# Sorting one block's neighbour lists and starting each layer with its first 16 slots

## The chip, the cores and the metric

The kernel runs on one core of a Trainium2 chip. The metric is the device time of one execution in microseconds. Engines are called by the profile's names: PE is TensorE, DVE is VectorE, ACT is ScalarE, POOL is GpSimd, and SP issues transfers only.

## The reference

Eight graphs (B = 8) share one random adjacency matrix of 2048 nodes with a density of 0.0078125, so about 16 neighbours a node; each node has 128 features. Four layers follow one another: two of attention with 8 heads over the neighbours, then two in which the weights come from a sum of two scores.

```python
x, adj = ...            # (8, 2048, 128), (2048, 2048)
# layers 0 and 1
scores = jnp.einsum('bnhd,bmhd->bhnm', Q, K) / jnp.sqrt(16.)
scores = jnp.where(mask, -jnp.inf, scores)        # mask: adj == 0
attn_out = softmax(scores) @ V
x = layer_norm(h + (attn_out @ Wo + bo))
x = layer_norm(x + relu(x @ W1 + b1) @ W2 + b2)
# layers 2 and 3
e = s_i[:, :, None] + s_j[:, None, :]             # s = (x @ W) @ a
e = jnp.where(e >= 0, e, 0.2 * e)
att = softmax(jnp.where(adj == 0, -jnp.inf, e))
x = layer_norm(att @ (x @ W) + x)
```

## The kernel before

A node needs only its neighbours' rows. In the start phase the kernel finds each node's neighbours, counts them, and sorts the nodes by falling count: `perm` holds the node at every place, `rank` the place of every node. The 2048 places make 16 blocks of 128 nodes (one node a partition). Block t has `CAPS[t]` neighbour slots, 28 in block 0 and 11 in block 15; the first 16 nodes of block 0 may have more, and 2 folded slots, spread over all partitions, take these. `find_lists` (L328) makes a block's list, by falling node number. `verdict` looks at all the limits at the end (`over` among them), and where one is broken, a general path computes everything anew.

Each layer l has a table in DRAM, `tables[l]`, with one row per node: keys and values of all 8 graphs for layers 0 and 1 (2048 numbers), features and two scores for layers 2 and 3 (1040). A slot of a block is one indirect DMA that GpSimd issues (`gather`, L299): 128 rows, one for each partition. Two slots make a chunk in layers 0 and 1, four in layers 2 and 3. Six buffers `kv0` to `kv5` hold chunks in turn; a chunk is fetched three chunks ahead of its use (four in layers 2 and 3: `AHEAD`).

A chunk of layers 0 and 1 is multiplied with the query on DVE (L528), reduced to scores (L531), turned into weights on ACT (L537), the values are multiplied on DVE (L542), and PE adds them into PSUM (L552). A chunk of layers 2 and 3 has small weight operations (L667 to L673), a multiply on DVE (L679), two of eight graphs on ACT (L684), an addition of pairs of slots (L688) and the sum on PE (L694).

When a block's last chunk is through, `outputs` (L565 or L571) multiplies the sums by the reciprocal of the weights' sums. Then the block's tail runs in two halves of four graphs each, on PE and ACT with one power on POOL for each norm (L411, in `normed`): projections and norms, then `project` computes the rows of the next layer's table, and `put_rows` (L419) writes them with an indirect DMA of POOL. `state_done` also stores the block's transposed state with a DMA of SP (L480) and starts the load (L295) of the state of the block three further on.

The order of the instructions on every engine is the order in which the program emits them. Tails are generators that give way at fixed points; each chunk's step has three slots, and in a slot every pending tail is taken one part further:

```python
def slot():
    advance(threads)
    advance(tails)
```

A layer ends with `drain`, which takes the tails to their end. Only then does the next layer's first fetch follow:

```python
for i in range(AHEAD[l]):
    fetch(i)
if l > 0:
    state(0)
drain()
begin(0)
drain()
```

Of the kernel before, what the change touches and what calls it, by code (L numbers as in the profile page):

```python
# [31 lines left out]
AHEAD = (3, 3, 4, 4)  # L32
# [6 lines left out]
CAPS = [BASE + FOLD, 23, 21, 20, 19, 18, 18, 17, 16, 16, 15, 14, 14, 13, 12, 11]  # L39
SEG = 128  # L40
# [12 lines left out]
def pieces(t, n):  # L53

    res, k = [], 0
    for m in split(CAPS[t] if t > 0 else BASE, n):
        res.append((k, m, False))
        k += m
    if t == 0:
        res.insert(1, (BASE, FOLD, True))  # L60
    return res
# [3 lines left out]
def sparse_path(ctx: ExitStack, tc: tile.TileContext, ins: dict, out: bass.AP, flag: bass.AP):  # L65
# [69 lines left out]
    first = [sum(CAPS[:t]) for t in range(NT)]  # L135

# [161 lines left out]
    def gather(l, at, dst):  # L298
        nc.gpsimd.indirect_dma_start(  # L299
            out=dst, out_offset=None, in_=tables[l][:, :],  # L300
            in_offset=bass.IndirectOffsetOnAxis(ap=lists[:, at : at + 1], axis=0),
            bounds_check=N - (l < 2), oob_is_err=False,
        )
# [72 lines left out]

    def folded_sums(w, box):
# [22 lines left out]
    def normed(z, dst):  # L400
# [15 lines left out]
        yield  # L416

# [56 lines left out]
    def state_done(l, t, box):  # L474
# [3 lines left out]
        if box["halves"] == 2:  # L478
# [3 lines left out]
            box["state"](t + 3)  # L482
# [257 lines left out]
    def start():  # L740
# [159 lines left out]
        nc.vector.tensor_add(perm, part1, pn[:, NT : 2 * NT])  # L900

# [35 lines left out]

    def advance(group):
        for g in list(group):
            if next(g, 0) == 0:  # L940
                group.remove(g)

    def slot():
        advance(threads)
        advance(tails)

# [5 lines left out]
    def tail(l, t, box):  # L952
        def rest():
            for _ in range(2 if l < 2 else 3):
                yield
            outputs(l, t, box)
            part = attention_tail if l < 2 else gat_tail
            tails.append(part(l, t, box, 0))
            tails.append(later(3, lambda: part(l, t, box, 4)))
            yield  # L960

        tails.append(rest())

# [5 lines left out]
    def layer(l):  # L969
        boxes = [{} for _ in range(NT)]  # L970
        att = l < 2
        per = 2 if att else 4
        chunks = []
        for t in range(NT):
            for k, ns, folded in pieces(t, per):
                chunks.append(dict(t=t, k=k, ns=ns, folded=folded, box=boxes[t], last=False))
            chunks[-1]["last"] = True
        n = len(chunks)

        def fetch(c):  # L980
            if c >= n:
                return
            c = chunks[c]
            c["buf"] = buffer()[:, : c["ns"] * width(l)].rearrange("p (s c) -> p s c", s=c["ns"])
            for i in range(c["ns"]):
                gather(l, first[c["t"]] + c["k"] + i, c["buf"][:, i])

        def state(t):
            if t < NT:
                if l == 0:  # L990
                    threads.append(fetch_state(t, boxes[t]))
                else:
                    boxes[t].update(x=load_state(t), ready=True)

        for box in boxes:
            box["state"] = state

        def begin(t):
            if att:
                threads.append(attention_begin(l, t, boxes[t]))  # L1000

        if l == 0:
            threads.append(find_lists(0))
            state(0)
            drain()
        for i in range(AHEAD[l]):
            fetch(i)
        if l > 0:
            state(0)
        drain()  # L1010
        begin(0)
        drain()
        if l == 0:
            threads.append(find_lists(1))
        run = [(attention_chunk if att else gat_chunk)(l, c) for c in chunks]

        def go(i, times=1):

            if 0 <= i < n:
                for _ in range(times):  # L1020
                    next(run[i], None)

        def is_last(i):
            return 0 <= i < n and chunks[i]["last"]

        def end(i):
            t = chunks[i]["t"]
            tail(l, t, chunks[i]["box"])

        for i in range(n + 2):  # L1030
            fetch(i + AHEAD[l])
            if i < n and chunks[i]["k"] == 0:
                t = chunks[i]["t"]
                if l == 0 and t + 2 < NT:
                    threads.append(find_lists(t + 2))
                if t == 0:
                    state(1)
                    threads.append(later(12, lambda: state(2) or iter(())))
                while att and "asked" not in chunks[i]["box"]:
                    advance(threads)  # L1040
            if i + 2 < n and chunks[i + 2]["k"] == 0:
                begin(chunks[i + 2]["t"])
            if att:

                go(i - 2)
                if is_last(i - 2):
                    end(i - 2)
                go(i)
                slot()
                go(i)  # L1050
                slot()
                if is_last(i - 1):
                    sums(l, chunks[i - 1]["t"], chunks[i - 1]["box"])
                go(i - 1, 2)
                slot()
            else:


                if i + 1 < n and chunks[i + 1]["folded"]:
# [544 lines left out]
```

## Time and profile before

| | |
|---|---|
| Time, median of 3 runs | 3458.94 us (3458.14 to 3458.99) |
| Span of the profiled execution | 3460.6 us |
| DVE busy | 3055.0 us, 88% |
| PE busy | 2749.7 us, 79% |
| POOL busy | 2125.4 us, 61% |
| ACT busy | 1435.0 us, 41% |
| Gathers (L299) | 1108, 1622.8 us on POOL |
| Power of the norm (L411) | 192, 318.2 us on POOL |
| Table writes (L419) | 48, 73.8 us on POOL |
| DMA, mean | 283 GB/s |

Busy times are sums over the whole span. Layers 0 and 1 take about 2100 us of it, layers 2 and 3 about 1180, and the stages have different limits, so the shares of the whole say little of any one of them. The time from a table's last write to the first use of its rows is seen in the timelines around 1217 to 1280 us, 2277 to 2340 and 2842 to 2889. POOL's records cover the issue of a gather, not its transfer.

### The profile page before, as it was taken

Reading aid. Unit: us, or ns where it says so; the run is one execution under the profiler, and the core shown is the slowest. Engines: PE = TensorE matmul, PEld = TensorE weight load, DVE = VectorE, ACT = ScalarE, POOL = GpSimd, SP = SyncE. Lnnn points to the kernel's source line nnn. Section 1 sums busy time; section 2 is a strip of 40 time slices with the busy share of each in tenths; the row PEclk is TensorE's granted clock in tenths of the full one; section 3 lists DMA queues with packets and bytes.
Section 4 is the critical chain, followed back from the end, with each engine's and each line's share of the span. In section 5 each row is a group of like instructions: output and inputs, shape, how many; then the busy total and the mean of one; then the engine's idle time right before and its main releaser. Section 6 shows DMA issues by size and latency. Waiting matters only on the chain. (4 is left out here: it accounts for less than half of the span.)

```text
span 3460.6 us, 34591 instructions
## 1 busy us (share of the span) xinstructions
PE 2749.7 (79%) x10618; PEld 1587.6 (46%) x10618; DVE 3055.0 (88%) x2685; ACT 1435.0 (41%) x4972; POOL 2125.4 (61%) x1441
## 2 busy tenths in 40 slices
PE   5657888799899966888888989975888995668675
PEld 4523455455555542444555556652444552223332
DVE  7789999999999929999999999938888875888886
ACT  5612333344344440233333434443555663444444
POOL 0053666666667533555677766628878756888874
PEclk9878999899999989989999999998999997988888
DMA  8486778888878547777887888729999967989883
GB/s 339 179 306 248 282 280 299 321 294 304 315 295 313 211 167 281 266 295 294 307 299 306 293 305 304 283 69 337 334 327 346 336 266 275 321 301 317 299 292 123
DMA packets 195887, 980.13 MB, mean 283 GB/s; under 512 B 28334, under 2 KB 30128, under 8 KB 124084
## 3 DMA queue, kind: packets, MB, share of 16 engines
q0 software_dynamic: 172352, 884.08, 70.2%
q1 hardware_dynamic: 18438, 75.51, 5.7%
q10 hardware_dynamic: 4904, 18.24, 1.4%
q8 instruction: 87, 1.43, 0.2%
q14 instruction: 106, 0.87, 0.1%
HBM read 937.13 MB, written 85.21 MB: 295 GB/s over the span
## 5 line engine op out<-in xcount | busy, mean ns | idle before, releaser
L299 POOL DMA_INDIRECT kv<-table,lists x1108 | 1622.8, 1465 | 523.7 <-issue 240.9
L552 PE MATMUL acc<-kv,ident 128*128 128x512 f32 x2200 | 1110.6, 636 | 257.7 <-DVE kv L542 257.4
L694 PE MATMUL acc<-kv,ident 128*128 128x512 f32 x1184 | 610.2, 664 | 236.7 <-DVE kv L688 191.1
L552 PEld LDWEIGHTS acc<-kv,ident 128*128 128x128 f32 x2200 | 413.4, 201 | 698.6 <-issue 368.2
L528 DVE TENSOR_TENSOR kv<-kv,q 128x2048 f32<-128x2048 f32 (+1 forms) x282 | 629.3, 2232 | 69.5 <-DMA kv<-table,lists 63.3
L531 DVE TENSOR_REDUCE sc<-kv 128x128 f32<-128x2048 f32 (+1 forms) x284 | 634.1, 2233 | 9.4
L411 POOL TENSOR_TENSOR rs<-ss,half 128x4 f32<-128x4 f32 x192 | 318.2, 1657 | 518.2 <-ACT n L406 517.1
L542 DVE TENSOR_TENSOR kv<-kv,w 128x2048 f32<-128x2048 f32 (+1 forms) x284 | 631.4, 2223 | 0.0
L406 ACT ACTIVATE n<-m,eps 128x128 f32<-128x128 f32 x768 | 271.9, 367 | 544.6 <-PE m L634 216.8
L694 PEld LDWEIGHTS acc<-kv,ident 128*128 128x128 f32 x1184 | 240.1, 213 | 543.3 <-issue 295.8
L679 DVE TENSOR_TENSOR kv<-kv,pair 128x3072 f32<-128x3072 f32 (+1 forms) x150 | 466.2, 3108 | 0.9
L684 ACT ACTIVATE kv<-kv,ws 128x128 f32<-128x128 f32 x1108 | 339.0, 403 | 189.2 <-DVE ws L673 86.8
L688 DVE TENSOR_TENSOR kv<-kv 128x2048 f32<-128x2048 f32 (+1 forms) x150 | 296.0, 1974 | 110.5 <-ACT kv L684 104.9
L537 ACT ACTIVATE w<-sc,lmask 128x64 f32<-128x64 f32 x554 | 164.6, 349 | 521.5 <-DVE sc L531 406.9
L415 ACT ACTIVATE n<-m,rs 128x128 f32<-128x128 f32 x768 | 219.6, 369 | 328.6 <-POOL rs L411 321.9
L406 ACT ACTIVATION_READ_ACCUMULATOR n<-m,eps 128x1 f32 x768 | 157.2, 205 | 0.0
L634 PE MATMUL m<-w_L_w,hT 128*128 128x128 f32 x1024 | 156.3, 275 | 0.0
L308 PE MATMUL m<-ident,n 128*128 128x128 f32 x640 | 105.9, 286 | 46.2 <-ACT n L415 45.7
L419 POOL DMA_INDIRECT table<-rows,perm x48 | 73.8, 1537 | 104.4 <-ACT rows L443 46.0
L634 PEld LDWEIGHTS m<-w_L_w,hT 128*128 128x128 f32 x1024 | 135.0, 192 | 0.0
L613 PE MATMUL m<-n1T,w_L_gnn_W 128*128 128x512 f32 x256 | 131.3, 597 | 3.3 <-ACT n1T L608 3.3
L308 PEld LDWEIGHTS m<-ident,n 128*128 128x128 f32 x640 | 81.6, 146 | 103.4 <-ACT n L415 49.9
(219 smaller groups left out, 3029.5 us busy)
## 6 DMA issues: line engine op xcount, KB each, us to landing
kept<-xT SPq DMA_DIRECT2D x48, 512.0 KB
xT<-kept SPq DMA_DIRECT2D x48, 512.0 KB
kv<-table,lists POOLq DMA_INDIRECT x1108
kv<-in_adj_dram SPq DMA_DIRECT2D x16, 1024.0 KB
table<-kv ACTq DMA_DIRECT2D x16, 1024.0 KB
kv<-in_x_nodes_dram SPq DMA_DIRECT2D x16, 512.0 KB
found<-cand POOLq DMA_DIRECT2D x16, 64.0 KB
table<-rows,perm POOLq DMA_INDIRECT x48
```

Of the source, the lines that this page charges most:

```text
L299: nc.gpsimd.indirect_dma_start(out=dst, out_offset=None, in_=tables[l][:, :], in_offset=bass.IndirectOffsetOnAxis(ap=lists[:, at : at + 1] ...
L406: nc.scalar.activation(dst[:, i, :], z[:, i, :], AF.Square, bias=eps, scale=D**-0.5, accum_out=ss[:, i : i + 1],)
L411: nc.gpsimd.tensor_tensor(rs, ss, half, op=ALU.pow)
L528: nc.vector.tensor_mul(kk, kk, q[:, None].to_broadcast([P, ns, NB, D]))
L531: nc.vector.tensor_reduce(sc[:, :ns].rearrange("p s (b h) -> p (s b) h", h=NH), kk.rearrange("p s b (h j) -> p (s b) h j", h=NH), axis=AX. ...
L542: nc.vector.tensor_mul(vv, vv, w[:, k : k + ns, :].rearrange("p s (b h) -> p (s b) h", h=NH)[:, :, None, :] .to_broadcast([P, ns * NB, HD, ...
L552: nc.tensor.matmul(acc[:, j, :], merge if c["folded"] else ident, kv[:, i, 4 * j : 4 * j + 4, D:], start=k + i == 0, stop=c["last"] and i ...
L634: nc.tensor.matmul(y[:, j, :], hT[:, f, j, :], wt["2"][:, f, :], start=False, stop=f == 1, skip_group_check=True,)
L679: nc.vector.tensor_mul(hv[:, :, :nv, :], hv[:, :, :nv, :], wc[:, :, :nv, None].to_broadcast([P, ns, nv, D]))
L684: nc.scalar.mul(hv[:, i, b, :], hv[:, i, b, :], ws[:, i, b - nv : b - nv + 1])
L688: nc.vector.tensor_add(hv[:, : ns - left], hv[:, : ns - left], hv[:, left:ns])
L694: nc.tensor.matmul(acc[:, j, :], merge if c["folded"] else ident, hv[:, i, 4 * j : 4 * j + 4, :], start=k + i == 0, stop=c["last"] and i = ...
```

## The change

One list of chunks, `every`, now runs through all four layers, and `layers` walks it without a drain between layers. `fetch` asks of each chunk how many blocks' rows must have been written to its layer's table (`put[l]`): all 16 as a rule. For block 0 of layers 1 to 3 there is a second list, `lists0`, with the same 28 neighbours ordered by their place in `perm`. Chunks within its first 8 slots ask for 14 blocks, chunks within its first 16 slots for 15. The folded chunk of these blocks moves from second place to behind slot 16.

`order_lists` makes `lists0` during layer 0, from block 2 on: `rank` is stored to DRAM in the start phase, 28 indirect gathers of one number per partition fetch the places (one a chunk), and DVE sorts keys made of place and node. Two more limits go into `over`: the 8th neighbour must not be in the last two blocks and the 16th not in the last one. `clear_late` writes zeros to the rows of blocks 14 and 15 in the tables of layers 1 to 3, with six `put_rows` during layer 0's first block.

`hurry` is true in block 15 of layers 0 to 2 and as long as a layer's table lacks rows that its chunks use; then a slot advances the tails twice. `state` passes from a layer's last blocks to the next layer's first, so these states are loaded as the blocks 13 to 15 are done. Where a chunk hasn't been fetched when its turn comes, slots go on without it until it has.

```diff
-AHEAD = (3, 3, 4, 4)
...
+EARLY = (8, 16)
...
-def pieces(t, n):
+def pieces(t, n, at):

     res, k = [], 0
     for m in split(CAPS[t] if t > 0 else BASE, n):
         res.append((k, m, False))
         k += m
     if t == 0:
-        res.insert(1, (BASE, FOLD, True))
+        res.insert(at, (BASE, FOLD, True))
...
+    lists0 = const.tile([P, BASE], I32, name="lists0")
+    ranks = dram.tile([N, 1], F32, name="ranks")
...
+    def order_lists():
+        place = small.tile([P, BASE], F32, tag="place", name="place", bufs=1)
+        nc.vector.memset(place, float(N))
+        for k in range(BASE):
+            nc.gpsimd.indirect_dma_start(
+                out=place[:, k : k + 1], out_offset=None, in_=ranks[:, :],
+                in_offset=bass.IndirectOffsetOnAxis(ap=lists[:, k : k + 1], axis=0),
+                bounds_check=N - 1, oob_is_err=False,
+            )
+            for _ in range(3):
+                yield
+        for _ in range(6):
+            yield
+        key = small.tile([P, 32], F32, tag="key", name="key", bufs=1)
+        nc.vector.memset(key, 0.0)
+        nc.vector.scalar_tensor_tensor(
+            key[:, :BASE], place, -4096.0, lists[:, :BASE], op0=ALU.mult, op1=ALU.subtract
+        )
+        nc.vector.tensor_scalar_add(key[:, :BASE], key[:, :BASE], float(4097 * N))
+        top = small.tile([P, 48], F32, tag="top", name="top")
+        for r in range(0, 32, 8):
+            nc.vector.max(top[:, r : r + 8], key)
+            if r < 24:
+                nc.vector.match_replace(key, top[:, r : r + 8], key, 0.0)
+        yield
+        for i, b in zip(EARLY, (2, 1)):
+            late = small.tile([P, 1], F32, tag="late", name="late", bufs=1)
+            nc.vector.tensor_single_scalar(
+                late, top[:, i - 1 : i], float(4096 * (b * P + 1)), op=ALU.is_lt
+            )
+            nc.vector.scalar_tensor_tensor(
+                over[:, 1, 0:1], top[:, i - 1 : i], late, over[:, 1, 0:1],
+                op0=ALU.mult, op1=ALU.max,
+            )
+        nc.vector.tensor_copy(lists0, top[:, :BASE])
+        nc.vector.tensor_single_scalar(lists0, lists0, 4095, op=ALU.bitwise_and)
+        nc.vector.tensor_scalar(
+            lists0, lists0, -1.0, float(N), op0=ALU.mult, op1=ALU.add
+        )
+        yield
...
+    def clear_late():
+        rows = rows_of(blocks[0][0])
+        nc.vector.memset(rows, 0.0)
+        for l in (1, 2, 3):
+            for t in (NT - 2, NT - 1):
+                for _ in range(3):
+                    yield
+                put_rows(l, t, rows)

...
+                put[l + 1] += 1
+            state(l, t + 3)

...
+        nc.sync.dma_start(ranks.rearrange("(t p) o -> p (t o)", p=P), rank)
...
+    put = [NT, 0, 0, 0]
+    every = []
+    blocks = [[{} for _ in range(NT)] for _ in range(4)]
+    for l in range(4):
+        per = 2 if l < 2 else 4
+        for t in range(NT):
+            for k, ns, folded in pieces(t, per, 1 if l == 0 else EARLY[1] // per):
+                c = dict(l=l, t=t, k=k, ns=ns, folded=folded, box=blocks[l][t], last=False)
+                c["run"] = (attention_chunk if l < 2 else gat_chunk)(l, c)
+                every.append(c)
+            every[-1]["last"] = True
+    now = [0, 0]
+    def fetch():
+        while now[1] < len(every):
+            c = every[now[1]]
+            l, t, k, ns = c["l"], c["t"], c["k"], c["ns"]
+            if now[1] - now[0] > (4 if now[1] >= KVB and every[now[1] - KVB]["l"] > 1 else 3):
+                return
+            need = NT
+            if l > 0 and t == 0 and not c["folded"]:
+                need -= (k + ns <= EARLY[0]) + (k + ns <= EARLY[1])
+            if put[l] < need:
+                return
+            c["buf"] = buffer()[:, : ns * width(l)].rearrange("p (s c) -> p s c", s=ns)
+            for i in range(ns):
+                if l > 0 and t == 0 and not c["folded"]:
+                    index = lists0[:, k + i : k + i + 1]
+                else:
+                    index = lists[:, first[t] + k + i : first[t] + k + i + 1]
+                gather(l, index, c["buf"][:, i])
+            now[1] += 1
+    def hurry():
+        c = every[min(now[0], len(every) - 1)]
+        return c["l"] < 3 and c["t"] == NT - 1 or c["l"] > 0 and put[c["l"]] < NT
     def slot():
         advance(threads)
         advance(tails)
+        if hurry():
+            advance(tails)
+        fetch()

...
+    def tail(l, t, box):
+        for _ in range(2 if l < 2 else 3):
+            yield
+        outputs(l, t, box)
+        part = attention_tail if l < 2 else gat_tail
+        n = 1 + hurry()
+        tails.append(later(n, lambda: part(l, t, box, 0)))
+        tails.append(later(n + 3, lambda: part(l, t, box, 4)))
+        yield
+    def state(l, t):
+        if t >= NT:
+            l, t = l + 1, t - NT
+        if l == 0:
+            threads.append(fetch_state(t, blocks[l][t]))
+        elif l < 4:
+            blocks[l][t].update(x=load_state(t), ready=True)
...
+    def layers():
+        threads.append(find_lists(0))
+        state(0, 0)
+        drain()
+        fetch()
+        begin(every[0])
+        drain()
+        threads.append(find_lists(1))
+        for i in range(len(every) + 2):
+            now[0] = i
+            fetch()
+            c2, c1, c, n1, n2 = (chunk(i + j) for j in range(-2, 3))
+            if c["k"] == 0:
+                l, t = c["l"], c["t"]
                 if l == 0:
+                    if t + 2 < NT:
+                        threads.append(find_lists(t + 2))
+                    if t == 0:
+                        state(0, 1)
+                        threads.append(later(12, lambda: state(0, 2) or iter(())))
+                        threads.append(later(12, clear_late))
+                    if t == 2:
+                        threads.append(order_lists())
+                while l < 2 and "asked" not in c["box"]:
+                    slot()
+            while i < len(every) and now[1] <= i:
                 slot()
+            if n2["k"] == 0:
+                begin(n2)
+            if c2["l"] in (0, 1):
+                go(c2)
+                if c2["last"]:
+                    threads.append(tail(c2["l"], c2["t"], c2["box"]))
+            if n1["l"] in (2, 3) and n1["folded"]:
+                go(n1)
+            if c1["l"] in (2, 3) and c1["last"]:
+                sums(c1["l"], c1["t"], c1["box"])
+            go(c)
+            slot()
+            go(c)
+            slot()
+            if c1["l"] in (0, 1) and c1["last"]:
+                sums(c1["l"], c1["t"], c1["box"])
+            go(c1, 2)
+            if c1["l"] in (2, 3) and c1["last"]:
+                threads.append(tail(c1["l"], c1["t"], c1["box"]))
+            slot()
+        verdict()
```

More of the change, by code (lines that the diff above doesn't have):

```diff
@@ L296, in load_state, with gather @@
         return xT
-    def gather(l, at, dst):
+    def gather(l, index, dst):
         nc.gpsimd.indirect_dma_start(
             out=dst, out_offset=None, in_=tables[l][:, :],
-            in_offset=bass.IndirectOffsetOnAxis(ap=lists[:, at : at + 1], axis=0),
+            in_offset=bass.IndirectOffsetOnAxis(ap=index, axis=0),
             bounds_check=N - (l < 2), oob_is_err=False,
@@ L481, in state_done @@
                 put_rows(l + 1, t, box["rows"])
-            box["state"](t + 3)
+                put[l + 1] += 1
+            state(l, t + 3)
     def attention_begin(l, t, box):
@@ L950, in drain @@
             advance(tails)
[L952 to L962, printed above, removed]
     def later(n, make):
@@ L967, in later @@
         yield from make()
[L969 to L989, printed above, removed]
-                if l == 0:
[L991 to L1048, printed above, removed]
-                slot()
[L1050 to L1059, printed above, removed]
-                    go(i + 1)
-                if is_last(i - 1):
-                    sums(l, chunks[i - 1]["t"], chunks[i - 1]["box"])
-                go(i)
-                slot()
-                go(i)
-                slot()
-                go(i - 1, 2)
-                if is_last(i - 1):
-                    end(i - 1)
-                slot()
-        if l == 3:
-            verdict()
@@ new lines, in begin, with chunk, go @@
+    def begin(c):
+        if c["l"] < 2:
+            threads.append(attention_begin(c["l"], c["t"], c["box"]))
+    def chunk(i):
+        return every[i] if 0 <= i < len(every) else dict(l=None, k=None, last=False, folded=False)
+    def go(c, times=1):
+        for _ in range(times if c["l"] is not None else 0):
+            next(c["run"], None)
+    def layers():
[12 more added lines that the diff above has]
+                l, t = c["l"], c["t"]
+                if l == 0:
+                    if t + 2 < NT:
[9 more added lines that the diff above has]
+            while i < len(every) and now[1] <= i:
+                slot()
+            if n2["k"] == 0:
[19 more added lines that the diff above has]
+        verdict()
@@ L1076, in sparse_path @@
         start()
-        for l in range(4):
-            layer(l)
+        layers()
 @with_exitstack
```

## The prediction

> **What bounds the kernel now.** I read the page's slices first, then VectorE's waits, then the timelines of VectorE and GpSimd at the places where VectorE is empty, and last the table by stage. The slices:
>
> ```profile
> DVE  7789999999999929999999999938888875888886
> DMA  8486778888878547777887888729999967989883
> ```
>
> VectorE is at nine tenths or more through layers 0 and 1 (slices 4 to 26) but for slice 15, where layer 1 begins; slices 27 and 34, with 3 and 5, are the other two changes of layer. The waits (total us, times, longest us) say what ends them:
>
> ```profile
> DVE kv L667 <- DMA kv<-table,lists: 98.8, 15, 53.6
> DVE kv L528 <- DMA kv<-table,lists: 63.3, 2, 53.1
> ...
> DVE o L571 <- PE acc L694: 19.5, 8, 9.1
> DVE o L565 <- PE acc L552: 17.0, 3, 8.3
> ```
>
> So in layers 0 and 1 VectorE waits for a gather twice in 2300 us, once for 53.1 us. VectorE's timeline at the first layer change, then at the other two (start us, us, ..., idle before):
>
> ```profile
> 1216.63 1.16 DVE L542 TENSOR_TENSOR kv<-kv,w 128x1024 f32<-128x1024 f32 x1
> 1226.06 1.23 DVE L565 TENSOR_TENSOR o<-acc,sums 128x1024 f32<-128x1024 f32 x1 [8.27 <-PE acc L552]
> 1280.38 2.29 DVE L528 TENSOR_TENSOR kv<-kv,q 128x2048 f32<-128x2048 f32 x1 [53.10 <-DMA kv<-table,lists]
> ...
> 2340.06 0.19 DVE L667 TENSOR_TENSOR kv<-kv,own 128x32 f32<-128x32 f32 x1 [53.59 <-DMA kv<-table,lists]
> ...
> 2889.15 0.19 DVE L667 TENSOR_TENSOR kv<-kv,own 128x32 f32<-128x32 f32 x1 [37.05 <-DMA kv<-table,lists]
> ```
>
> VectorE is empty 8.3 + 53.1 = 61.4 us at the first edge (call it A), 8.1 + 53.6 = 61.7 at B, 9.1 + 37.1 = 46.1 at C: 169 us in all. GpSimd's timeline shows what fills A:
>
> ```profile
> 1239.18 1.01 POOL L411 TENSOR_TENSOR rs<-ss,half 128x4 f32<-128x4 f32 x1 [7.57 <-ACT n L406]
> 1240.37 1.04 POOL L419 DMA_INDIRECT table<-rows,perm  x1 [0.18 <-issue]
> 1243.58 1.04 POOL L411 TENSOR_TENSOR rs<-ss,half 128x4 f32<-128x4 f32 x1 [2.17 <-ACT n L406]
> 1251.19 1.01 POOL L411 TENSOR_TENSOR rs<-ss,half 128x4 f32<-128x4 f32 x1 [6.57 <-ACT n L406]
> 1256.45 1.01 POOL L411 TENSOR_TENSOR rs<-ss,half 128x4 f32<-128x4 f32 x1 [4.25 <-ACT n L406]
> 1263.33 1.03 POOL L419 DMA_INDIRECT table<-rows,perm  x1 [5.87 <-ACT rows L443]
> 1271.44 1.04 POOL L299 DMA_INDIRECT kv<-table,lists  x1 [7.08 <-DMA table<-rows,perm]
> ```
>
> Block 14's rows go to the table at 1240.4, block 15's at 1263.3, 37 us after its output multiply; they land 8.1 us later, and the first chunk is complete 8.9 us after that. By stage (us, PE, PEld, DVE, ACT, POOL busy, clock, DMA share, GB/s):
>
> ```profile
> 440.00:560.00 120.00, 98.21 (x362) 56.51 (x362) 118.60 (x72) 37.83 (x121) 77.39 (x45) 0.90 0.86 325
> 1160.00:1226.00 66.00, 61.65 (x270) 38.64 (x271) 51.61 (x32) 31.76 (x104) 24.16 (x15) 0.97 0.36 135
> 1226.00:1263.00 37.00, 30.56 (x191) 23.93 (x189) 1.23 (x1) 23.75 (x81) 6.11 (x6) 1.00 0.16 61
> ```
>
> Inside layer 0 VectorE sets the pace (118.6 of 120) and GpSimd and the DMA engines have some room. At the edge TensorE is nearly full (61.7 of 66).
>
> **What the skill says.** "DMA: Bandwidth & Descriptors", section "Two DMAs through the same engine are not ordered": an issuing engine must wait for the first DMA's completion before it issues one that reads its bytes. The trace agrees: GpSimd stands 7.08 us ahead of the gather at 1271.44. The same page, "Anatomy of one DMA — SWDGE (gpsimd) path", puts one transfer at 2.0 us plus bytes over 436 GB/s, most of the constant being the write's receipt: 4.4 us for 1 MB of rows. The trace has 8.1 from issue, which I use. "SBUF — State Buffer", section "SBUF: two separate sides": a GpSimd operation and some VectorE operations exclude each other for an instruction's length. The trace fits: gathers take 0.99 us beside an idle VectorE, up to 3.0 beside a busy one.
>
> **The change, part by part.** The build gives GpSimd's new order at A: put 13, one gather, a power, chunk 0's gathers, a power, chunk 1's, two powers, chunk 2's, put 14, chunks 3 to 5, a power, chunk 6, a power, chunk 7, two powers, put 15, the folded chunk. (A put is a block's table write, a power is L411; dependences are by whole table, so every gather behind a put waits until it has landed, and every put waits for all gathers before it.)
>
> *Edge A.* Before, eight chunks at VectorE's pitch of 6.72 us (1291.63 to 1298.35) from 1280.4 end at 1334. After, they begin when block 15 ends, 1217.8. Put 13 was at 1206.5; with tails advanced twice a slot I put it at 1195, landed 1203, chunk 0 there by 1212: no wait. Put 14 comes after its two powers, about 1227 against 1240.4, landed 1235; chunk 3, behind it on the queue though it needs no row of it, arrives at 1244 and is wanted at 1238: 5 us lost. Block 15's tail now shares TensorE with eight chunks (four matmuls in 1.71 us each, 13.7 in all) and layer 1's first query (3.5); the gaps of 37 - 30.6 = 6.4 us take part: 1263.3 + 13.7 + 3.5 - 6.4 = 1274. By the chain of powers it would be 1266 to 1272. I take 1272, landed 1280, folded chunk there at 1289; VectorE is done with its eight at 1217.8 + 53.8 + 1.2 + 5 = 1278. Gain 1334 - 1289 = 45. Ends: 54 if the tail isn't slowed, 30 if put 15 slips to 1287.
>
> *Edge B.* Layer 2's first 16 slots are four chunks. There the gathers set the pace: they leave GpSimd back to back, 1.3 us apart. Counting these: 16, the folded two and the next four, the 22nd ended at 2360.3. After: put 14 at about 2289 (2300.35 before), landed 2297; chunks 2 and 3 issue to 2307.5; block 15's first power, at 2299.2 before, stands behind those eight gathers until 2307.5, the second at 2308.7 against 2303.1, so put 15 moves from 2322.2 to 2328, lands 7.7 later at 2335.5, and six gathers end at 2343. Gain 17. Ends 5 and 24.
>
> *Edge C.* The tail is shorter and both of block 14's and block 15's first powers stand behind eight gathers that wait for a put. Put 13 at 2837 (2844.5), landed 2842, eight gathers to 2852.5; block 14's powers there instead of at 2843.3 and 2848.7; put 14 at 2865 (2860.9), landed 2870; eight gathers to 2881; block 15's powers at 2881 to 2883 against 2859.8 and 2863.5; put 15 at 2893.5 (2873.6), landed 2899, six gathers to 2907. Before, the 22nd ended at 2911.3. Gain 4, ends -8 and 15.
>
> *Added on VectorE in layer 0*, where it is the bound: zeroing 128x2048 (128x128 takes 165 ns, 128x192 218; by the slope 1.7 us, at most the 2.28 of a multiply of that size); four maxima of at most 0.29, three replacements of at most 0.28 + 0.09, two small memsets and ten small operations of about 0.17: 3.5 us. Together 5 (4 to 6), nothing hides it.
>
> *Added on GpSimd in layer 0*: 28 gathers of one number a partition, one a chunk, and six zero-row puts among the gathers of block 0. GpSimd holds 77.4 us and 45 gaps of 0.25 in 120 us, so 31 us are free, 1.7 in a pitch of 6.72. No trace row is such a gather; the nearest is the list gather L331 (mean 1.68 in this stage, 0.97 at best) and 0.3 ahead: 1.3 to 2.0 each. Chunks are fetched three ahead, 20 us of cover. The puts fall at 200 to 250 us, where the DMA share is 0.93 at 352 GB/s (0.66 in the next 50): their 4.2 MB are 12 us of DMA, 3.5 find room there, and part of the rest eats into the chunks fetched ahead. I take 4 us for the puts and 3 for the place gathers; ends 0 (all covered) and 33 (8, and 28 x 0.9 short).
>
> *Costed at nothing*: the place store on SP (8 KB, read only two blocks later), first states now loaded as earlier blocks finish, behind the store of block 13 on SP and some 13 us before use; the folded chunk's later place; the 16 slots' order inside a sum; the dropped drains, counted in the edges.
>
> Sum: 45 + 17 + 4 - 5 - 7 = 54. Against the span of 3460.6 that is 3406.6; the timed runs lie 1.7 lower (3458.94), so 3405.
>
> **The rivals.** *The waits return.* The puts' landings hold GpSimd's queue and with it the powers of the tails they wait for; then A gives 30, B 5, C -8, less 15: 12 us, 3447. For it: the build's order; against: at A TensorE, not the powers, is late. *All is hidden.* A 54, B and C 16 gathers x 1.6 = 26 each, less 10: 3363. Against: the put of block 15 still has its own chain of 37 us. *GpSimd becomes the bound in layer 0, ending slower.* A place gather is 128 separate numbers of 4 bytes; if it holds its queue over 1.7 us a pitch, kv gathers fall behind, and after 20 us VectorE stands. The 66 us of edge gains less 12 are used up when each takes (54 + 20) / 28 + 1.7 = 4.3 us; at 5 us the time is 3459 + 28 x 3.3 - 20 - 54 = 3477. *It doesn't do it*: were a neighbour among a row's first 8 in the last two blocks, or among 16 in the last, the general path would run instead. By the reference's inputs the 8th has place 1265 at most (limit 1792), the 16th 1788 (1920): left out but for 1 in 100.
>
> **How the numbers follow.** Forecast 0.68, all hidden 0.10, waits return 0.15, GpSimd bound 0.06, other path 0.01. A measurement tells about 0.2%, 7 us, from no change. The forecast and the hidden case are faster; of the waits' case 0.11 is, 0.03 the same and 0.01 slower: 0.89, 0.03, 0.08. The forecast's own ends, its terms not all at their worst together, are about 3382 and 3430; the range 3374 to 3440 adds the nearer part of both neighbours.
>
> **What would show it.** VectorE's gap at A gone before the first chunk of layer 1, and one of 5 to 20 us ahead of the folded chunk; at B and C a gap that stands behind four chunks; block 15's powers later after its output multiply than the 13 us of before; layer 0 longer by 8 to 16 us. Wrong if VectorE waits for gathers inside layer 0 for over 20 us, if C gains over 15, or if put 15 at A comes after 1290.

## The result, and the profile after

The changed kernel takes 3469.84 us (median of 20 runs), the kernel before 3459.93 us beside it: ratio 1.0028, 95% interval 1.002 to 1.0036. It is slower by 10 us, a little over what a measurement can tell; 3405 us and "faster" were predicted. The profiled spans are 3466.6 and 3460.6 us, so 6.0 of the 10 us can be followed in the profiles.

From the changed kernel's page, its slices of VectorE:

```profile
DVE  7789999999999969999999999937888865888885
```

At A the hole has gone from 2 to 6; at B (3 and 7) and C (6 and 5) there is as much hole as before. The changed kernel's waits of VectorE (total us, times, longest us); its value multiply is L601, its q multiply L587, the output multiplies are L624 and L630:

```profile
DVE kv L726 <- DMA kv<-table,lists: 103.4, 13, 41.2
DVE kv L601 <- ACT w L596: 29.3, 4, 12.7
DVE o L630 <- PE acc L753: 26.9, 11, 7.7
DVE kv L587 <- DMA kv<-table,lists: 21.3, 3, 9.6
```

The q multiply's wait for gathers fell from 63.3 to 21.3 us: that is A. The wait of layers 2 and 3 for gathers has not fallen (98.8, now 103.4), and a wait is new: value multiplies that stand for ScalarE's exponentials (L596), 29.3 us in four places, all at the edges. VectorE's timeline at A, then B, then C:

```profile
1222.43 2.29 DVE L601 TENSOR_TENSOR kv<-kv,w 128x2048 f32<-128x2048 f32 x1 [8.57 <-ACT w L596]
1228.19 2.29 DVE L587 TENSOR_TENSOR kv<-kv,q 128x2048 f32<-128x2048 f32 x1 [3.47 <-ACT q L565]
1234.87 1.37 DVE L438 TENSOR_REDUCE sums<-w 128x64 f32<-128x704 f32 x1 [2.07 <-ACT w L596]
1258.41 2.29 DVE L587 TENSOR_TENSOR kv<-kv,q 128x2048 f32<-128x2048 f32 x1 [5.56 <-DMA kv<-table,lists]
...
2261.34 2.29 DVE L601 TENSOR_TENSOR kv<-kv,w 128x2048 f32<-128x2048 f32 x1 [12.75 <-ACT w L596]
2290.44 0.19 DVE L726 TENSOR_TENSOR kv<-kv,own 128x32 f32<-128x32 f32 x1 [9.20 <-DMA kv<-table,lists]
2343.59 0.18 DVE L726 TENSOR_TENSOR kv<-kv,mine 128x16 f32<-128x16 f32 x1 [41.20 <-DMA kv<-table,lists]
...
2841.88 0.19 DVE L726 TENSOR_TENSOR kv<-kv,own 128x32 f32<-128x32 f32 x1 [12.30 <-DMA kv<-table,lists]
2862.59 1.23 DVE L630 TENSOR_TENSOR o<-acc,sums 128x1024 f32<-128x1024 f32 x1 [7.67 <-PE acc L753]
2873.26 0.19 DVE L726 TENSOR_TENSOR kv<-kv,own 128x32 f32<-128x32 f32 x1 [9.44 <-DMA kv<-table,lists]
2909.36 0.18 DVE L726 TENSOR_TENSOR kv<-kv,mine 128x16 f32<-128x16 f32 x1 [24.16 <-DMA kv<-table,lists]
```

The one long gap of each edge is cut into several short ones, and the one ahead of the folded chunk ("kv<-kv,mine") is left: 41.2 us at B, where A's is 6.1 us.

Where the time went can be read block by block: the start of a block's output multiply, changed kernel less kernel before. The difference is +5.2 us through layer 0 (3.3 of them come between blocks 3 and 4, where the lists are sorted), -25.5 in layer 1, -17.9 at the first block of layer 2, -1.9 at the first of layer 3, +1.1 at the last block, and +6.0 at the end of the span. I call the step over an edge (from block 13 of the old layer to block 0 of the new) the edge's gain: A 30.7, B -7.6, C -17.7. Then 5.2 - 30.7 + 7.6 + 17.7, less 1.7 won inside layer 2, plus 3.0 inside layer 3 and 4.9 after the last output multiply, are the 6.0 us. Edges at which a kernel below has nothing early read between -2.9 and +3.2: take 3 us as what this reading can't tell. With early chunks A is less steady: e2_flush and e8_spread below run the same program there and read 26.2 and 31.9, e10_two_edges and e11_three_edges 23.5 and 28.8; take 6 us there.

What holds B is seen on GpSimd and ScalarE. The changed kernel's GpSimd timeline there, and its puts of blocks 14 and 15:

```profile
2236.13 1.04 POOL L459 TENSOR_TENSOR rs<-ss,half 128x4 f32<-128x4 f32 x1 [5.28 <-ACT n L454]
2237.37 3.06 POOL L304 DMA_INDIRECT kv<-table,lists  x1 [0.19 <-issue]
2240.73 1.83 POOL L304 DMA_INDIRECT kv<-table,lists  x1 [0.30 <-PE m L313]
2242.86 0.99 POOL L304 DMA_INDIRECT kv<-table,lists  x1 [0.30 <-PE m L672]
2244.16 2.91 POOL L304 DMA_INDIRECT kv<-table,lists  x1 [0.30 <-issue]
2247.09 1.14 POOL L459 TENSOR_TENSOR rs<-ss,half 128x4 f32<-128x4 f32 x1
...
2273.10 1.94 POOL L477 DMA_INDIRECT table<-rows,perm  x1 [7.02 <-ACT rows L528]
2330.32 1.05 POOL L477 DMA_INDIRECT table<-rows,perm  x1 [5.23 <-ACT rows L528]
```

The kernel before has its put of block 15 here:

```profile
2322.17 1.03 POOL L419 DMA_INDIRECT table<-rows,perm  x1 [5.22 <-ACT mine L657]
```

Counted from the output multiply of block 13 (2178.4 and 2203.9), block 15's put comes at 151.9 us in the changed kernel, at 118.2 in the one before: 33.7 us later.

ScalarE meanwhile:

```profile
2239.92 0.21 ACT L454 ACTIVATION_READ_ACCUMULATOR n<-m,eps 128x1 f32 x1
...
2248.27 1.14 ACT L463 ACTIVATE n<-m,rs 128x128 f32<-128x128 f32 x4 [6.42 <-POOL rs L459]
...
2256.71 0.37 ACT L454 ACTIVATE n<-m,eps 128x128 f32<-128x128 f32 x1 [5.51 <-PE m L693]
...
2260.74 0.57 ACT L596 ACTIVATE w<-sc,lmask 128x64 f32<-128x64 f32 x2
```

The squares for the second power are done at 2240.1; the power (L459) runs at 2247.1, behind chunk 0's four gathers. ScalarE's scaling (L463) waits for it, TensorE for that, ScalarE's next squares (L454) for TensorE, and behind all of it in ScalarE's order stand block 15's last exponentials (L596), at 2260.7. VectorE, which wants them, is empty 12.75 us in the middle of block 15. At C eight gathers in a row (2830.75 to 2841.92) stand ahead of block 14's power at 2841.95. Block 15's weights are summed by then (VectorE ends them at 2829.6); what is held there is TensorE, in whose order block 15's last sums stand behind block 14's tail.

### The profile page after: what moved, and what is told of

Its sections match the earlier page's. It is cut to its first block, busy times and chain, and to the rows that moved or that the text cites. A ratio compares the mean times of both kernels' runs of the same rounds, so it can differ in the third digit from the quotient of the medians.

```text
span 3466.6 us, 34648 instructions
## 1 busy us (share of the span) xinstructions
PE 2763.2 (80%) x10618; PEld 1590.5 (46%) x10618; DVE 3059.9 (88%) x2707; ACT 1431.0 (41%) x4972; POOL 2221.3 (64%) x1475
## 4 chain that ended last, share of the span: by engine, by line
DVE 36%; PE 22%; issue 19%; DMA 9%; POOL 6%; ACT 4%; POOLq 0%; DVEq 0%; ACTq 0%
DVE kv L601 12%; DVE kv L587 12%; PE acc L611 7%; DMA kv<-table,lists 7%; PE acc L753 5%; POOL kv L304 4%; DVE kv L747 2%; DVE sc L590 2%; DVE kv L738 2%; PE m L693 2%; DVE sums L438 1%; POOL rs L459 1%; PE m L672 1%; ACT kv L743 1%; PE m L313 1%
## 5 line engine op out<-in xcount | busy, mean ns | idle before, releaser
L601 DVE TENSOR_TENSOR kv<-kv,w 128x2048 f32<-128x2048 f32 (+1 forms) x284 | 631.3, 2223 | 29.3 <-ACT w L596 29.3
L587 DVE TENSOR_TENSOR kv<-kv,q 128x2048 f32<-128x2048 f32 (+1 forms) x282 | 629.1, 2231 | 20.1 <-DMA kv<-table,lists 15.2
L459 POOL TENSOR_TENSOR rs<-ss,half 128x4 f32<-128x4 f32 x192 | 325.5, 1695 | 419.9 <-ACT n L454 418.4
L454 ACT ACTIVATE n<-m,eps 128x128 f32<-128x128 f32 x768 | 272.2, 368 | 543.2 <-PE m L693 219.8
L463 ACT ACTIVATE n<-m,rs 128x128 f32<-128x128 f32 x768 | 219.5, 370 | 378.9 <-POOL rs L459 378.6
L596 ACT ACTIVATE w<-sc,lmask 128x64 f32<-128x64 f32 x554 | 165.0, 351 | 481.2 <-DVE sc L590 371.5
L477 POOL DMA_INDIRECT table<-rows,perm x54 | 91.6, 1696 | 155.7 <-ACT rows L528 67.1
L454 ACT ACTIVATION_READ_ACCUMULATOR n<-m,eps 128x1 f32 x768 | 158.0, 206 | 0.0
```

The costliest lines, as they stand in the source:

```text
L454: nc.scalar.activation(dst[:, i, :], z[:, i, :], AF.Square, bias=eps, scale=D**-0.5, accum_out=ss[:, i : i + 1],)
L459: nc.gpsimd.tensor_tensor(rs, ss, half, op=ALU.pow)
L587: nc.vector.tensor_mul(kk, kk, q[:, None].to_broadcast([P, ns, NB, D]))
L601: nc.vector.tensor_mul(vv, vv, w[:, k : k + ns, :].rearrange("p s (b h) -> p (s b) h", h=NH)[:, :, None, :] .to_broadcast([P, ns * NB, HD, ...
```

## The experiments

All kernels compute the whole of the reference. They come from the changed kernel by a few switches: SOON names the layers with early chunks, FLUSH the layers ahead of which the old layer is ended first, TWICE_IN and TWICE_ON the edges at which tails are advanced twice a slot, while block 15 runs and while the table lacks rows. The switches move the lines by 4 (gather L308, power L463, exponentials L600). The first columns are edge gains in us, an edge with nothing early in parentheses; the next say how much later than in the kernel before block 15's rows are put, counted from block 13's output multiply. The kernel before took 3461.1 to 3461.3 us beside the experiments:

| kernel | A | B | C | put later: A | B | C | us |
|---|---|---|---|---|---|---|---|
| changed | 30.7 | -7.6 | -17.7 | 25.4 | 33.7 | 42.6 | 3469.84 |
| e1_once | 20.7 | -15.3 | -21.5 | 36.1 | 41.3 | 45.2 | 3491.18 |
| e2_flush | 26.2 | 0.4 | -9.0 | 18.2 | 26.4 | 34.8 | 3457.46 |
| e3_first_edge | 30.2 | (2.6) | (-2.7) | 25.8 | 0.0 | 0.0 | 3446.43 |
| e4_added_only | (3.2) | (2.8) | (-2.4) | -1.4 | 0.0 | 0.0 | 3476.51 |
| e5_tail_order | 29.8 | (2.2) | (-2.6) | 26.3 | 0.0 | 0.0 | 3439.98 |
| e6_twice_late | 20.9 | -7.3 | -1.0 | 23.7 | 33.5 | 25.1 | 3463.52 |
| e7_no_work | (-1.2) | (0.6) | (0.5) | 2.9 | 0.0 | 0.0 | 3468.82 |
| e8_spread | 31.9 | 7.6 | -2.3 | 15.1 | 19.4 | 28.3 | 3439.56 |
| e9_spread_only | 30.1 | -1.9 | -9.6 | 25.4 | 27.0 | 35.7 | 3458.46 |
| e10_two_edges | 23.5 | 6.9 | (-2.9) | 20.6 | 20.6 | 0.0 | 3439.20 |
| e11_three_edges | 28.8 | 7.7 | 1.0 | 15.3 | 19.4 | 24.6 | 3433.06 |
| e12_rows_only | (3.2) | (-2.1) | (1.7) | -1.5 | 2.6 | 0.0 | 3467.20 |

One thing decides B and C in all these kernels: when block 15's rows are put. Where an edge has early chunks, its gain and the delay of that put add up to 25 to 27.5 us at B (eight kernels) and to 24 to 26 us at C (seven), whatever was changed. At A the sum is 55.5 to 57 without the flush and 44 to 47 with it: in e2_flush the eighth early chunk's gathers there stand behind the put as well.

**e1_once**: no tail is advanced twice.

```diff
-        if hurry():
-            advance(tails)
```

> Tails are advanced once a slot everywhere, all else as in the changed kernel. Theory 1 (order: the doubled tails put ACT and PE instructions that still wait ahead of the next chunks' exponentials, and block 15's output multiply stands on VectorE behind the new layer's first two chunks): VectorE's waits for the exponentials, 29 us in four waits after the change, fall below 10; but the puts of blocks 14 and 15 come later in the order, so the time moves by only -10 to +5 us against the changed kernel, 3460 to 3475. Theory 2 (queue: gathers that wait for a put hold the powers behind them on GpSimd): the same gathers stand before the same powers, the exponential waits stay within 5 us of 29, time 3467 to 3473.

Measured: 3491.18 us, ratio 1.0083 [1.007, 1.0096]. VectorE's waits for exponentials fell as theory 1 had it: of 29.3 us at the value multiplies and 7.8 at the weights' sums, 3.1 us at the sums are left. Yet the kernel is worse than the changed one by 21 us, at each edge, and neither theory had that. The waits come with the double advance, but it is no burden to be taken off: without it block 15's rows come still later.

**e2_flush**: two empty entries between the layers, so that block 15 is ended and its output multiply emitted ahead of the next layer's first chunk.

```diff
+        if l in (1, 2, 3):
+            for _ in range(2):
+                every.append(dict(l=None, k=None, last=False, folded=False))
```

> Between two layers the steps of the old layer's last two chunks and the output multiply of its block 15 are emitted before the new layer's first chunk; gathers ahead, early slots and doubled tails stay. Theory 1: the output multiply of block 15 returns to 8 to 12 us after the block's last value multiply at the second and third edge (after the change it came 16 and 34 us later against the block's pace), block 15's table write comes 37 to 45 us after it in layer 1 and about 25 in layer 2, and the time falls to 3430 to 3448. Theory 2: the powers still stand behind eight gathers that wait for a table write, block 15's writes at the second and third edge move by under 10 us, and the time stays at 3460 to 3472.

Measured: 3457.46 us, ratio 0.9987 [0.998, 0.9994]: 12.4 us back, between the ranges of the two theories. B and C get 8.0 and 8.7 us back; A reads 4.5 us less. VectorE's timeline of e2_flush at B shows what is left:

```profile
2273.02 2.29 DVE L605 TENSOR_TENSOR kv<-kv,w 128x2048 f32<-128x2048 f32 x1 [12.30 <-ACT w L600]
2282.39 1.36 DVE L442 TENSOR_REDUCE sums<-w 128x64 f32<-128x704 f32 x1 [7.08 <-ACT w L600]
2289.51 1.23 DVE L628 TENSOR_TENSOR o<-acc,sums 128x1024 f32<-128x1024 f32 x1 [3.71 <-PE acc L615]
```

The output multiply now stands ahead of the early chunks, but 19 us of waits for exponentials are ahead of it. The order on VectorE is one cause of two.

**e3_first_edge**: early chunks and double advance at A alone.

```diff
-SOON, FLUSH, TWICE_IN, TWICE_ON = (1, 2, 3), (), (1, 2, 3), (1, 2, 3)
+SOON, FLUSH, TWICE_IN, TWICE_ON = (1,), (2, 3), (1,), (1,)
```

> Early slots and doubled tails at the first edge only; at the second and third the old layer is ended first and every gather waits for all 16 blocks, as before the change. By the edges' own balance in the two traces (first edge 31 us gained, layer 0 5 us lost, second 8 and third 18 lost): 3430 to 3440 under theory 1 and theory 2 alike. Rival: what the first edge gains is given back later by work that is only shifted: 3450 to 3462.

Measured: 3446.43 us, ratio 0.9958 [0.9944, 0.9973]. A alone makes the kernel faster than before by 14.7 us, between the two ranges. The shortfall, 6 to 16 us, led to the next.

**e4_added_only**: nothing early, nothing doubled; what is left of the change is its added work and its new order of threads.

```diff
-SOON, FLUSH, TWICE_IN, TWICE_ON = (1, 2, 3), (), (1, 2, 3), (1, 2, 3)
+SOON, FLUSH, TWICE_IN, TWICE_ON = (), (1, 2, 3), (), ()
```

> No early slots, no doubled tails, every layer ended before the next; what stays of the change is the place store, the 28 place gathers, the sort, the zero rows, the next layer's first states loaded earlier, and tails run among the other threads. By layer 0's balance (5.2 us): 3463 to 3467. Rival: what is added also costs at the end of layer 3, where the trace lost 3 to 6 us more: 3468 to 3472.

Measured: 3476.51 us, ratio 1.004 [1.0027, 1.0053]: 15.4 us over before, three times the 5.2 that I expected and past the rival's range too. Block by block it is +7.2 in layer 0, +1.5 at block 11 of layer 3, +8.1 at block 15, +13.0 at the end.

**e7_no_work**: e4_added_only without places, sort and zeroed rows.

```diff
-                        threads.append(later(12, clear_late))
-                    if t == 2:
-                        threads.append(order_lists())
...
-        nc.sync.dma_start(ranks.rearrange("(t p) o -> p (t o)", p=P), rank)
```

> The kernel of e4_added_only (nothing early, nothing doubled) without its added work: no places, no sorted lists, no zeroed rows put into the tables. Its instructions then are in the order of before, but for layer 1's first queries, which are asked for a little earlier, and the output multiplies of layer 3, which stand ahead of the block before's final multiplies. Theory: added work costs 5 to 8 us and stays in layer 0, the order of layer 3 costs the other 5 to 10: 3466 to 3470 us. Rival, all of it is the added work: 3460 to 3463 us. Rival, all of it is order: 3474 to 3478 us.

Measured: 3468.82 us, ratio 1.0025 [1.0016, 1.0035], as the theory had it: 7.6 us over before are order, the 7.7 to e4_added_only are added work. All that now differs from before in the engines' orders is layer 1's first query and, in layer 3, where the output multiply stands. The change starts `tail` among the threads, which a slot advances ahead of the tails. VectorE's timeline of the kernel before, late in layer 3, and then of the changed kernel:

```profile
3411.46 0.69 DVE L729 TENSOR_TENSOR n<-n,last_g 128x512 f32<-128x512 f32 x1
3412.18 0.69 DVE L730 TENSOR_TENSOR n<-n,last_b 128x512 f32<-128x512 f32 x1
3412.79 1.22 DVE L571 TENSOR_TENSOR o<-acc,sums 128x1024 f32<-128x1024 f32 x1
```

```profile
3412.56 1.22 DVE L630 TENSOR_TENSOR o<-acc,sums 128x1024 f32<-128x1024 f32 x1
3413.70 0.68 DVE L788 TENSOR_TENSOR n<-n,last_g 128x512 f32<-128x512 f32 x1
3414.41 0.69 DVE L789 TENSOR_TENSOR n<-n,last_b 128x512 f32<-128x512 f32 x1
```

The final multiplies of the block before now stand behind the next block's output multiply, and behind its wait for TensorE where it has one.

**e5_tail_order**: e3_first_edge with `tail` among the tails where tails are advanced once. The edit is the same in both places that start a `tail`, and the tail's halves then start 0 or 2 slots after it, not 1 or 2.

```diff
-                threads.append(tail(c1["l"], c1["t"], c1["box"]))
+                (threads if hurry() else tails).append(tail(c1["l"], c1["t"], c1["box"]))
```

> The kernel of e3_first_edge (early chunks and doubled tails at edge A alone), with each block's tail back among the tails, as before the change, so that in layer 3 VectorE does the final multiplies of the block before ahead of the next block's output multiply. Theory: the 5 to 6 us that every variant so far lost over layer 3's last four blocks, and part of the 5 us from the last output multiply to the end, come from that order: 3436 to 3441 us, and the offset to before does not move from block 11 to block 15 of layer 3. Rival: they come from the added work (lists, places, zeroed rows) or from the clock, and the order is nothing: 3445 to 3448 us, as e3_first_edge.

Measured: 3439.98 us, ratio 0.9939 [0.9925, 0.9952]: 6.5 us from the order, and the offset from block 11 to block 15 of layer 3 stays (-23.1, -22.9), where e3_first_edge loses 4.8 us (-27.2, -22.4). The theory holds.

**e12_rows_only**: e7_no_work with the zeroed rows put back.

```diff
+                        threads.append(later(12, clear_late))
```

> The kernel of e7_no_work with the zeroed rows put into the tables again, but no places and no sorted lists: it splits the 7.7 us between e7_no_work (3468.8) and e4_added_only (3476.5). Theory, the six puts of zeroed rows cost nothing in layer 0 and are the 3.6 us that every kernel with the added work shows between its last put and the end (15.5 us against 12.0), the sort is the rest in layer 0: 3471 to 3474 us, last put to end 15.5 us. Rival, the end comes from the sort's gathers: 3468 to 3470 us, last put to end 12.0 us.

Measured: 3467.20 us, ratio 1.0016 [1.0009, 1.0022]; last put to end 12.7 us. The rival was nearly right, 0.8 us under its range: the zeroed rows cost nothing that the times show, and the place store, the place gathers and the sort 9.3 us (3476.51 - 3467.20). Of these 3.3 are the sort in layer 0 and some 3 come after the last put, where every kernel with the sort shows 15.4 to 15.8 us to the end and those without it 11.9 to 12.7; the rest is not placed. What takes longer there is in the last section.

**e6_twice_late**: e2_flush, but tails are doubled only once block 15's own chunks are through.

```diff
-SOON, FLUSH, TWICE_IN, TWICE_ON = (1, 2, 3), (1, 2, 3), (1, 2, 3), (1, 2, 3)
+SOON, FLUSH, TWICE_IN, TWICE_ON = (1, 2, 3), (1, 2, 3), (), (1, 2, 3)
```

> The kernel of e2_flush (early chunks at all three edges, the old layer ended first), but the tails are not doubled while block 15's own chunks run, only after them, as long as the next table lacks rows. Theory: the doubled tails put instructions that wait for TensorE and GpSimd ahead of the last chunks' exponentials on ScalarE, which stopped VectorE for 12.3 and 7.1 us at edge B of e2_flush; without them these two waits are under 3 us each, the output multiply of block 15 comes as early as before, B and C give 5 to 15 us each more: 3435 to 3448 us. Rival: block 14's tail then ends later, its put keeps the third early chunk and the other gathers behind it, and what is won before the output multiply is lost after it: 3455 to 3470 us.

Measured: 3463.52 us, ratio 1.0006 [0.9998, 1.0014]: the rival's range. At B one wait of 11.8 us for the exponentials is left of e2_flush's 12.3 and 7.1, where the theory had two under 3, and VectorE then waits 8.8 us for TensorE's sums, not 3.7. The theory, that the doubling in block 15 is what stops the exponentials, holds at most in part, and block 15's rows come 7.1 us later at B. The doubling in block 15 wins 5 us at A and 8 at B and loses 8 at C.

**e8_spread**: e2_flush, with gathers of layers 2 and 3 one to a slot while the table lacks rows.

```diff
-            for i in range(ns):
+            for i in range(c.get("got", 0), ns):
...
+                c["got"] = i + 1
+                if l > 1 and put[l] < NT and i + 1 < ns:
+                    return
```

> The kernel of e2_flush, but while a table lacks rows the gathers of layers 2 and 3 are issued one at a time, one at each slot of the program, and not four in a row, so that a normalization's power on GpSimd stands behind one gather (about 1.3 us) and not four (6 to 10 us). Theory: at B and C the powers behind the gathers hold ScalarE, TensorE and with them the last exponentials and the tail of block 15: the put of block 15 comes 5 to 8 us earlier at each, 3442 to 3452 us. Rival: the doubled tails' instructions themselves stand in the way, whatever GpSimd does: 3454 to 3461 us, and VectorE still waits 10 us or more for the exponentials at B.

Measured: 3439.56 us, ratio 0.9942 [0.9929, 0.9956]: 17.9 us less than e2_flush, more than the theory asked. GpSimd's timeline of e8_spread at the place shown above:

```profile
2236.52 1.04 POOL L463 TENSOR_TENSOR rs<-ss,half 128x4 f32<-128x4 f32 x1 [5.28 <-ACT n L458]
2237.75 3.05 POOL L308 DMA_INDIRECT kv<-table,lists  x1 [0.19 <-issue]
2240.83 2.14 POOL L463 TENSOR_TENSOR rs<-ss,half 128x4 f32<-128x4 f32 x1
```

And VectorE's there:

```profile
2254.13 2.29 DVE L605 TENSOR_TENSOR kv<-kv,w 128x2048 f32<-128x2048 f32 x1 [5.15 <-ACT w L600]
2263.50 1.36 DVE L442 TENSOR_REDUCE sums<-w 128x64 f32<-128x704 f32 x1 [7.08 <-ACT w L600]
```

The power runs behind one gather, 6.3 us sooner (block 14's output multiply, 2225.2, is within 0.4 us of the changed kernel's), and the first wait for exponentials is 5.15 instead of 12.3 us. The second stays. Counted from block 13's output multiply, block 15's put comes at 137.7 us, against 144.6 in e2_flush, 151.9 in the changed kernel and 118.2 before. At C it is block 15's last sums on TensorE that come sooner; VectorE's output multiply in e2_flush, then in e8_spread:

```profile
2863.07 1.22 DVE L634 TENSOR_TENSOR o<-acc,sums 128x1024 f32<-128x1024 f32 x1 [24.21 <-PE acc L757]
```

```profile
2840.03 1.23 DVE L634 TENSOR_TENSOR o<-acc,sums 128x1024 f32<-128x1024 f32 x1 [17.59 <-PE acc L757]
```

**e9_spread_only**: the edit of e8_spread on the changed kernel, with FLUSH = ().

> The changed kernel with one edit: while a table lacks rows, layers 2 and 3 issue one gather at each slot instead of four in a row (the edit of e8_spread, without the flush of e2_flush). Theory, the row of four gathers ahead of the powers costs by itself what it cost in e8_spread against e2_flush (17.9 us): 3450 to 3456 us. Rival, without the flush the output multiply of block 15 still stands behind the new layer's first chunks on VectorE and decides: 3462 to 3470 us, with the put of block 15 at B less than 5 us earlier than in the changed kernel.

Measured: 3458.46 us, ratio 0.9988 [0.998, 0.9997]: 11.4 us, between the two ranges. At B block 15's put is at 145.2 us on the count above, 6.7 better. VectorE's timeline of e9_spread_only at B (the second line is the output multiply):

```profile
2275.86 2.29 DVE L751 TENSOR_TENSOR kv<-kv 128x2048 f32<-128x2048 f32 x1
2278.06 1.22 DVE L628 TENSOR_TENSOR o<-acc,sums 128x1024 f32<-128x1024 f32 x1
```

The output multiply has no wait of its own: it is held by a chunk of layer 2 ahead of it. So at B the flush gives 8.0 us, single gathers 5.7, both 15.2; at C 8.7, 8.1 and 15.4. Two causes, nearly additive at the edges; in the times they give 12.4, 11.4 and 30.3 us.

**e10_two_edges** and **e11_three_edges**: flush, single gathers and the tails' order together, with early chunks at A and B, and at all three; the first differs from the second by

```diff
-SOON, FLUSH, TWICE_IN, TWICE_ON = (1, 2, 3), (1, 2, 3), (1, 2, 3), (1, 2, 3)
+SOON, FLUSH, TWICE_IN, TWICE_ON = (1, 2), (1, 2, 3), (1, 2), (1, 2)
```

> The flush, the gathers one at a slot and the tails among the tails (as in e5_tail_order), with early chunks at edges A and B alone; C as before. From e8_spread (3439.6 us) minus 6.4 us that the tail's order gave in e5_tail_order, and minus the 2.3 us that e8_spread lost between the first blocks of layer 2's end and layer 3's start: 3429 to 3435 us. If the gains do not add up, 3436 us or more.

> The kernel of e10_two_edges with early chunks at C too. Theory, C stays a loss of 0 to 3 us even with the flush and single gathers: 3430 to 3437 us, slower than e10_two_edges by 0 to 4 us. Rival, C gains what the prediction gave it (4 us): 3425 to 3430 us.

Measured: e10_two_edges 3439.20 us, ratio 0.9934 [0.9921, 0.9947]; e11_three_edges 3433.06 us, ratio 0.9916 [0.9903, 0.9929]. The first is in the range named for gains that don't add up, the second in the theory's but is the faster one, against it; it is e8_spread with the tails' order, which gives 6.5 us again. The intervals overlap; in the profile C reads +1.0 against -2.9 without early chunks, in e8_spread -2.3. C is a small gain or none. Why A reads only 23.5 in e10_two_edges isn't explained; e11_three_edges has the same program there. e11_three_edges is the fastest kernel here, 28 us under before and 37 under the changed one. Its slices of VectorE:

```profile
DVE  7789999999999968999999999966888876888895
```

## Why the prediction was wrong

**A: predicted 45, measured 30.7 (its lower end was 30).** Put 13 at 1195.5 is what was said; put 14 came at 1241.4, not 1227, and put 15 at 1293.9, past the 1290 that I named as refuting. The step that failed is the time of put 15: 8.7 us later than before by the sum, 25.4 as measured from block 13's output multiply. Two terms of it were off.

First, the step "chunks begin when block 15 ends" took block 15's end as unmoved. Its output multiply comes 18.9 us later (1244.9 against 1226.1), 5.2 of them layer 0's. For the other 13.7, 11.3 us of the new layer's chunks now stand ahead of it on VectorE, and VectorE's waits after block 13 come to 16.2 us where they were 14.1. Second, TensorE's term has half of the matmuls: "four matmuls in 1.71 us" are one slot, and a chunk has two. In the changed kernel a chunk's eight stand in a row:

```profile
1245.06 3.70 PE L611 MATMUL acc<-kv,ident 128*128 128x512 f32 x8 [2.46 <-DVE kv L601]
```

At the prediction's 1.71 us for four, eight chunks are 27.4 us and not 13.7, and its sum gives 1288 for put 15. That is near what was measured, but it is one reading: TensorE is busy 46 of the 50 us from 1190 to 1240 and most of ScalarE's waits there end with it, yet no experiment here parts TensorE's load from the order on the other engines. The 5 us for chunk 3 behind put 14 (5.56) came out right by luck: it was wanted at 1252.9 and came at 1258.4, both some 14 us later than said.

**B: predicted +17, measured -7.6; C: predicted +4, measured -17.7.** The failing step is where put 15 was costed: 6 us later at B, for block 15's powers behind gathers alone, and 20 at C; measured were 33.7 and 42.6. With the measured delays in their place, the prediction's sums give 28 at A, -11 at B and -19 at C, against 30.7, -7.6 and -17.7, so the rest of its working held. Two terms were missing. First, in the changed kernel block 15's output multiply stands on VectorE behind the new layer's first chunks, which at C wait for gathers behind a put (the 12.30 us at 2841.88): 8.0 us at B and 8.7 at C (e2_flush). The diff shows it: `go(c)` of the new layer runs two or three slots ahead of the old layer's `tail`. Second, I did hold powers behind gathers, but only block 15's at B and, at C, as a delay of puts alone. Block 14's powers, behind a row of gathers, hold ScalarE and TensorE, and so the exponentials of block 15 itself at B and its last sums at C: 7.2 and 6.7 us more on top of the flush (e8_spread), 5.7 and 8.1 without it. With both taken away B gives 7.6 and C about nothing: the direction of the prediction, B at the low end of its range. The rest of B's shortfall is not settled: put 15 is still 19.4 us later than before, and VectorE's second wait of 7.1 us for exponentials stays in e8_spread.

**Layer 0.** VectorE's added work: predicted 5; the added instructions last 5.2 us (zeroing 1.76, the sort 3.4). That the changed kernel's offset through layer 0 is 5.2 too is partly luck: the other kernels with the sort, which run the same program there, read 6.5 to 12.8. Puts and place gathers: predicted 7, measured nothing that shows: VectorE has no new wait for gathers there, with 28 place gathers of 1.9 us (median) on GpSimd; by that scatter a few us can't be excluded.

**Costed at nothing.** The list had no line for the new place of `tail`, and it costs 6.5 us in layer 3 (e5_tail_order), nor for the end of the program, where 3.7 us are added. As the edges' gain (30.7 - 7.6 - 17.7) and layer 0's 5.2 us about cancel, those two are most of what the kernel lost.

**The rivals.** "The waits return" named the cause, GpSimd's queue ahead of the tails' powers, and a fall to B 5 and C -8; it was right in kind and 22 us short in size, since it had no term for VectorE's order, for the new place of `tail` or for the end. So my chance of 0.08 for slower rested on ends that left that term out.

## What to carry to other kernels

When work of the next stage is put beside the tail of the last, follow each in-order engine through the tail's whole chain: what the early work puts ahead of the tail's small steps decides, even on an engine with room to spare. Where the early work stands ahead of the old stage's last step on the bound engine, as at B and C, end the old stage first (at A that won nothing), and issue early gathers one at a time, so that a small operation of the chain stands behind one of them and not behind four. A helper that starts work among another list of threads moves it on every engine and in every stage; compare the order in stages that the change isn't about.

## What was not expected of the hardware

The time from the last put's issue (in layer 3 it writes the output's rows) to the end of the span is 11.9 to 12.7 us in the kernels without the 28 place gathers and the sort, and 15.4 to 15.8 in those with them, though that work ends near 602 us of 3466. The difference is in GpSimd's closing instructions INC_SWDGE_SEM and DRAIN: 1.60 and 5.79 us with the 1220 indirect DMAs of the kernel before and e7_no_work, 1.72 and 6.28 with the 1226 of e12_rows_only, 2.28 and 8.57 with the 1254 of every other kernel. The drains of GpSimd's sequencer (POOLq; ns, shortest, median and longest) in these three, the changed kernel last:

```profile
L1593 POOLq DRAIN  x3: 40/107/5790, 3453.9 to 3460.3; - x3
L1674 POOLq DRAIN  x3: 40/107/6280, 3460.4 to 3467.2; - x3
L1660 POOLq DRAIN  x3: 40/107/8567, 3457.2 to 3466.3; - x3
```

So each added indirect DMA, put of zeros or place gather, added 0.10 us at the end (0.61 for 6, 3.46 for 34). The first 1220 can't have cost that much each; why these do isn't shown. And the same instructions of layer 0 came out 5.2 to 12.8 us longer than before's from one profiled execution to another (changed kernel and e2_flush), so that spans of single profiles are compared edge by edge here, not as wholes.
